# Attention scores of an adjacency-masked network in four 32-column tiles of 96 moving columns

## Chip, cores and metric

The kernel runs on one core of one Trainium2 chip. The metric is the device time of the core in microseconds (us), the median of several executions. Before the change it is 2836.74 us (three runs, 2836.55 to 2839.01).

## What is computed

A pre-norm residual around two layers of masked attention over 128 batches of 64 tokens with 768 features, all in f32:

```python
h = relu(layernorm(x))                              # x: 128 x 64 x 768
for l in range(2):
    m_left, m_right = h @ W_left[l].T, h @ W_right[l].T
    u_left, u_right = h @ m_left^T / sqrt(768), h @ m_right^T / sqrt(768)       # 64 x 64 per batch
    u = u_left * triu(adj) + u_right * triu(adj, 1)^T
    e = exp(u) * adj
    attention = e / (e.sum(2) + 1e-10)
    h = relu(layer_norm(attention @ (h @ W_lin[l].T + b_lin[l])))
out = x + h
```

The left scores are only used on and above the diagonal, the right ones only below it. Half of all score products are thrown away by the mask.

## The kernel before

Each layer has a first pass (left and right projections, scores, softmax) and a second (the linear projection and the attention product). A pass works through 16 stages of 8 batches. In a stage of the first pass, `project` runs 2 x 15 steps of matmuls; after the first step of stage u, `scores(u - 1)` puts a burst of 48 matmuls into the stream of TensorE. What follows on the other engines is cut into tasks, one per half step ("slot"), and `softmax` gives the chain of the scores seven slots. X, Y, Z and V in the profile are the PSUM banks in which the projections are summed, m their copy in SBUF.

```python
def softmax(u):
    return [lambda: next(CHAIN[u], None)] * 7

def project(u, k, just):
    ...
    for i, (at, t, _) in ...:                       # 15 steps
        ...
        for g in range(2):
            for c in range(K2):
                nc.tensor.matmul(p[:, g], w[ORDER[i][0]][:, c, g * P:(g + 1) * P], b()[t][:, c, :], ...)
            if g == 0:
                run(30 * k + 2 * i)                 # tasks of this slot
        if i == 0 and k == 0:
            if u:
                scores(u - 1)
            ...
        read(...)                                   # ACT or DVE takes the bank into m
        run(30 * k + 2 * i + 1)

def scores(u):
    ht, m, adj = HT[1, l, u], M[u], ADJ[u]
    p = ps_aux.tile([P, 2, T], F32, name="aux")[:, 0].rearrange("p (q m) -> p q m", q=Q)
    for q in range(Q):                              # 4 pairs of batches
        for c in range(C):                          # 6 blocks of 128 features
            for h in range(PAIR):                   # 2 batches: column tiles 0-63 and 64-127
                b = q * PAIR + h
                nc.tensor.matmul(p[h * S:(h + 1) * S, q, :], ht[:, c, b * S:(b + 1) * S],
                                 m[:, c, b].rearrange("p k j -> p (k j)"),
                                 start=(c == 0), stop=(c == C - 1))

    def chain():
        wm = sp.tile([P, Q, 2, S], F32, name="wm", bufs=1)
        for k in range(2):                          # adjacency times triangle, on POOL
            nc.gpsimd.tensor_tensor(wm[:, :, k], adj[:, :, 1 - k], tri[:, k]..., op=ALU.mult)
        yield
        flat = wm.rearrange("p q k j -> p (q k j)")
        nc.vector.tensor_tensor(flat, p.rearrange("p q m -> p (q m)"), flat, op=ALU.mult)
        yield
        v = adj[:, :, 0, :]
        nc.vector.tensor_add(v, wm[:, :, 0], wm[:, :, 1])
        yield
        nc.scalar.activation(v, v, AF.Exp, scale=ISTEMPER)
        yield
        ...                                         # times adj, row sums, division, transpose, to DRAM
    CHAIN[u] = chain()
```

The moving data of one matmul are 128 columns: 64 of the left projection, then 64 of the right.

## Time and profile before

| | before |
|---|---|
| time, median | 2836.74 us |
| profiled span | 2835.8 us |
| TensorE busy | 2790.3 us, 98% |
| VectorE (DVE) busy | 1288.6 us, 45% |
| scores (L378): 32 bursts, each | 5.588 us |
| one stage of the first pass | 57.39 us |

A busy TensorE says nothing of gaps inside its stream: its matmuls are pipelined, so their durations overlap, and what they cost is read from their start times. The lines of the page on which the argument rests stand in the prediction. The view of the scores' line (in the second line: total idle us before its records and how often):

```profile
  issue: 10.6, 32
```

One wait of about 0.33 us per burst: that is the entry, where the array changes from 128-column to 64-column tiles (the view takes weight loads and matmuls together; here it is the loads that wait). From the page's list of DMA queues (packets, MB, share of 16 engines):

```profile
q8 instruction: 125, 2.05, 0.3%
```

### The profile page before, as it was taken

The page shows a single profiled execution, that of the slowest core. Times are in us where ns is not written, and L with a number is a line of the kernel's source. Part 1 is how long each engine was busy: PE and PEld are TensorE (multiplying, and loading weights), DVE is VectorE, ACT ScalarE, POOL GpSimd, SP SyncE. Part 2 cuts the span into 40 slices and gives each one's busy share as a digit, 9 for nine tenths or more (in the row PEclk, how much of TensorE's full clock was granted, in tenths as well). Part 3 has the DMA queues.
Part 4 walks back from the last instruction along what each step waited for, and adds up shares of the span by engine and source line. Part 5 has one row for each costly group of instructions (what it writes and reads, how often), then busy time and mean ns, then how long its engine had stood idle before and what let it go on. Part 6 is the DMA issues. An engine that isn't in the chain of part 4 may idle for free.

```text
span 2835.8 us, 39864 instructions
## 1 busy us (share of the span) xinstructions
PE 2790.3 (98%) x15640; PEld 2382.8 (84%) x15640; DVE 1288.6 (45%) x2126; ACT 839.6 (30%) x1453; POOL 1189.4 (42%) x935
## 2 busy tenths in 40 slices
PE   7999999999999999999999999999999999999997
PEld 6888888888888888888778888888888888888885
DVE  6454444444444333332334434343334334666666
ACT  2122222322231244444422221112111224544443
POOL 3343333222322556565422343223322325787875
PEclk9999999999999999999999999999999999999999
DMA  5622443234322243343553432344224304555654
GB/s 155 165 73 73 103 111 77 73 94 119 78 73 75 97 141 117 101 129 104 147 158 88 117 87 73 78 116 97 73 73 103 93 25 127 160 178 160 180 162 125
DMA packets 234043, 310.40 MB, mean 109 GB/s; under 512 B 54144, under 2 KB 184448, under 8 KB 225664
## 3 DMA queue, kind: packets, MB, share of 16 engines
q1 hardware_dynamic: 233568, 307.06, 39.6%
q8 instruction: 125, 2.05, 0.3%
q10 hardware_dynamic: 288, 0.79, 0.1%
q14 instruction: 62, 0.51, 0.1%
HBM read 202.91 MB, written 104.86 MB: 109 GB/s over the span
## 4 chain that ended last, share of the span: by engine, by line
PE 95%; DVE 1%; issue 1%; POOL 1%; ACT 1%; DMA 0%; SPq 0%; DVEq 0%; ACTq 0%; POOLq 0%
PE X L356 23%; PE V L356 15%; PE X L614 12%; PE Y L356 11%; PE Z L356 8%; PE V L614 8%; PE aux L378 6%; PE Y L614 6%; PE Z L614 4%; PE aux L544 3%; POOL w_r L144 1%; DVE m L144 0%; DVE w_l L144 0%; DMA x<-in_x_dram 0%; DVE hl L144 0%
## 5 line engine op out<-in xcount | busy, mean ns | idle before, releaser
L144 POOL TENSOR_TENSOR ts<-ht 128x512 f32<-128x512 f32 x441 | 585.5, 1338 | 1244.6 <-DMA ht<-h 594.5
L189 ACT ACTIVATE m<-X 128x512 f32<-128x512 f32 x256 | 152.8, 597 | 1154.7 <-PE X L356 591.3
L144 POOL TENSOR_TENSOR ts<-ht,ts 128x512 f32<-128x512 f32 x189 | 248.8, 1324 | 156.0 <-PE X L614 78.2
L144 DVE TENSOR_TENSOR m<-m,V 128x512 f32<-128x512 f32 x256 | 174.7, 682 | 283.5 <-PE V L356 282.4
L144 DVE TENSOR_TENSOR m<-m,X 128x512 f32<-128x512 f32 x256 | 163.7, 680 | 274.8 <-PE X L356 274.8
L144 DVE TENSOR_TENSOR m<-m,Z 128x512 f32<-128x512 f32 x128 | 88.0, 687 | 377.1 <-ACT m L189 308.8
L356 PE MATMUL X<-ts,w_l 128*128 128x256 f32 x1024 | 246.1, 384 | 9.7 <-ACT m L189 5.1
L614 PE MATMUL X<-w_n,ts 128*128 128x256 f32 x1024 | 244.0, 380 | 4.1 <-ACT hl L189 3.9
L356 PE MATMUL X<-ts,w_r 128*128 128x256 f32 x1024 | 241.9, 379 | 0.0
L356 PEld LDWEIGHTS X<-ts,w_l 128*128 128x128 f32 x1024 | 194.9, 192 | 40.6 <-issue 6.3
L614 PEld LDWEIGHTS X<-w_n,ts 128*128 128x128 f32 x1024 | 191.7, 190 | 35.0 <-ACT hl L189 4.7
L356 PEld LDWEIGHTS X<-ts,w_r 128*128 128x128 f32 x1024 | 192.3, 190 | 28.7
L255 ACT ACTIVATE ht<-ht,b_col,a_col 128x512 f32<-128x512 f32 x192 | 143.1, 803 | 153.2 <-DMA ht<-h 153.2
L614 PE MATMUL Y<-w_n,ts 128*128 128x256 f32 x768 | 182.4, 379 | 0.0
L356 PE MATMUL Y<-ts,w_l 128*128 128x256 f32 x768 | 181.8, 380 | 0.0
L356 PE MATMUL Y<-ts,w_r 128*128 128x256 f32 x768 | 181.4, 379 | 0.0
L189 ACT ACTIVATE hl<-X 128x512 f32<-128x512 f32 (+1 forms) x136 | 77.7, 572 | 332.7 <-PE X L614 323.1
L378 PEld LDWEIGHTS aux<-m,ht 128*64 128x64 f32 x3072 | 167.0, 137 | 10.6 <-issue 10.6
L378 PE MATMUL aux<-m,ht 128*64 128x128 f32 x3072 | 174.7, 274 | 0.0
L356 PEld LDWEIGHTS Y<-ts,w_l 128*128 128x128 f32 x768 | 146.3, 191 | 20.0
L356 PEld LDWEIGHTS Y<-ts,w_r 128*128 128x128 f32 x768 | 145.9, 190 | 19.8
L614 PEld LDWEIGHTS Y<-w_n,ts 128*128 128x128 f32 x768 | 145.9, 190 | 19.8
(105 smaller groups left out, 4563.1 us busy)
## 6 DMA issues: line engine op xcount, KB each, us to landing
ht<-h SPq DMA_DIRECT2D x63, 1536.0 KB, 7.3
h<-xb SPq DMA_DIRECT2D x124, 384.0 KB, 6.5
z<-z SPq DMA_DIRECT2D x128, 192.0 KB, 2.9
x<-z SPq DMA_DIRECT2D x128, 192.0 KB, 8.5
xr<-in_x_dram SPq DMA_DIRECT2D x128, 192.0 KB, 3.9
out_dram<-xr SPq DMA_DIRECT2D x128, 192.0 KB, 2.7
x<-in_x_dram SPq DMA_DIRECT2D x120, 192.0 KB, 8.5
adj<-in_adj_dram SPq DMA_DIRECT2D x64, 128.0 KB, 2.8
```

The source lines that it names most:

```text
L144: (eng.tensor_add if sign == "+" else eng.tensor_sub)(o, a, b)
L189: nc.scalar.activation(to(o), p, AF.Copy, scale=1.0 if sign == "+" else -1.0)
L255: nc.scalar.activation(ht, ht, AF.Relu, bias=cols[1][:, c:c + 1], scale=cols[0][:, c:c + 1])
L356: nc.tensor.matmul(p[:, g], w[ORDER[i][0]][:, c, g * P:(g + 1) * P], b()[t][:, c, :], start=(new and g == c == 0), stop=(c == K2 - 1), ski ...
L378: nc.tensor.matmul(p[h * S:(h + 1) * S, q, :], ht[:, c, b * S:(b + 1) * S], m[:, c, b].rearrange("p k j -> p (k j)"), start=(c == 0), stop ...
L544: nc.tensor.matmul(cx[k][i, m, :HH], at[j, q, :], hl[j, q, m * HH:(m + 1) * HH], start=True, stop=True)
L614: nc.tensor.matmul(p[:, n], b[t][:, c, r * P:(r + 1) * P], w[s][:, c, :], start=(i in FIRST and i not in PRELOAD and n == c == 0), stop=(c ...
```

## The change

Of the 128 moving columns, rows 0 to 31 of a batch need columns 0 to 95 (all left scores, right ones below token 32), and rows 32 to 63 need columns 32 to 127. So each 64-column tile is cut into two 32-column tiles with 96 moving columns each: a quarter of the products goes. The mask product must then leave out the PSUM columns that were never written, which differ from one 32-partition part to the next, so it becomes four products, and the chain takes an eighth slot. (In `wm` those columns are already zero.)

```diff
             def softmax(u):
-                return [lambda: next(CHAIN[u], None)] * 7
+                return [lambda: next(CHAIN[u], None)] * 8
 ...
-                            nc.tensor.matmul(p[h * S:(h + 1) * S, q, :], ht[:, c, b * S:(b + 1) * S],
-                                             m[:, c, b].rearrange("p k j -> p (k j)"),
-                                             start=(c == 0), stop=(c == C - 1))
+                            mb = m[:, c, b].rearrange("p k j -> p (k j)")
+                            for e in (0, 32):
+                                nc.tensor.matmul(p[h * S + e:h * S + e + 32, q, e:e + 96],
+                                                 ht[:, c, b * S + e:b * S + e + 32], mb[:, e:e + 96],
+                                                 start=(c == 0), stop=(c == C - 1))
 ...
-                    nc.vector.tensor_tensor(flat, p.rearrange("p q m -> p (q m)"), flat, op=ALU.mult)
-                    yield
+                    for i in range(0, P, 32):
+                        r = wm.rearrange("p q k j -> p q (k j)")[i:i + 32, :, i % S:i % S + 96]
+                        nc.vector.tensor_tensor(r, p[i:i + 32, :, i % S:i % S + 96], r, op=ALU.mult)
+                        if i % S:
+                            yield
```

## The prediction

> **What bounds the kernel now.** I began with the busy table and the 40 slices of the page, then took the chain that ended last.
>
> ```profile
> PE 2790.3 (98%) x15640; PEld 2382.8 (84%) x15640; DVE 1288.6 (45%) x2126; ACT 839.6 (30%) x1453; POOL 1189.4 (42%) x935
> ...
> PE 95%; DVE 1%; issue 1%; POOL 1%; ACT 1%; DMA 0%; SPq 0%; DVEq 0%; ACTq 0%; POOLq 0%
> PE X L356 23%; PE V L356 15%; PE X L614 12%; PE Y L356 11%; PE Z L356 8%; PE V L614 8%; PE aux L378 6%; PE Y L614 6%; PE Z L614 4%; PE aux L544 3%; POOL w_r L144 1%; DVE m L144 0%; DVE w_l L144 0%; DMA x<-in_x_dram 0%; DVE hl L144 0%
> ```
>
> TensorE carries 95% of the chain; everything else runs beside it. The scores (aux, L378) are 6% of it. So a microsecond taken from the scores is a microsecond of the end time, and DVE time counts only where it delays a PSUM bank that TensorE wants back. The ceiling is low: all scores cost 6%, and the change removes a quarter of their columns.
>
> The groups by line and the views of single lines give the operations touched:
>
> ```profile
> L378 PE MATMUL aux<-m,ht x3072: 272/273/324, 84.4 to 2349.3; 128*64 128x128 f32 x192
> L544 PE MATMUL aux<-hl,at x1024: 482/482/534, 979.0 to 2822.2; 64*64 64x384 f32 x171
> L390 DVE TENSOR_TENSOR wm<-aux,wm x32: 681/683/693, 115.0 to 2349.7; 128x512 f32<-128x512 f32 x32
> L393 DVE TENSOR_TENSOR adj<-wm x32: 419/424/426, 115.7 to 2350.4; 128x256 f32<-128x256 f32 x32
> ```
>
> A matmul's 273 ns is a pipelined latency, not its cost. The cost is in the start times, so I read the timeline of TensorE around one of the 32 scores bursts:
>
> ```profile
> 369.69 1.89 PE L356 MATMUL X<-ts,w_l 128*128 128x256 f32 x8
> 371.51 5.46 PE L378 MATMUL aux<-m,ht 128*64 128x128 f32 x96
> 376.90 1.99 PE L356 MATMUL Z<-ts,w_l 128*128 128x256 f32 x8
> ```
>
> 48 matmuls of the program are 96 records (two per f32 matmul). Record by record, inside a burst they start in pairs, one in each 64-column tile: 7 ns between the two, 102 ns to the next pair, so 109.3 ns a pair. A 256-column matmul on the whole array starts every 215.9 ns, and the four 64x64 tiles of the context (L544, 384 columns) start 6.7 ns apart and repeat every 322.6 ns. The three lie on one line: period = 2.6 ns + 0.8333 ns x columns, whether one, two or four tiles are at work. The entry costs 93 ns (309 ns from the last X start instead of 216) and 51 ns at the second pair; leaving costs 93 and 104 ns. Altogether each burst adds 5.588 us between X and the second Z matmul (48 x 109.3 ns + 0.34 us), and all 32 bursts agree within 1 ns. In a steady stage of the first pass (57.388 us from burst to burst) no other gap appears.
>
> **What the Trainium skill says.**
> - "TensorE: Matmul & The Clock Gate", section "Measured speedup vs the span model": column tiles of 32 and row tiles run concurrently, about 4 ns per further tile; a full 4x4 packing is listed with 10.6 times. The trace agrees in kind with 6.7 to 7 ns per tile, for two and four tiles. It holds no 32-column tile and no four column tiles.
> - "TensorEngine Tiling (Array Packing)", section "Key Properties": a change of tiling mode drains the array. The trace agrees: about 0.3 us a burst, and the change keeps it, one entry and one exit per burst.
> - The same page, section "Instruction Overhead": about 60 cycles per matmul, so a small moving size stops paying. At 96 columns we are above this, and the trace's own fixed term is 2.6 ns.
> - "VectorE: DVE Perf Modes", section "The TRN2 errata — SBUF-src ops pay a fixed extra latency per instruction": an f32 tensor_tensor takes (N+151)/0.96 ns, N per partition. That gives 691 and 424 ns for 512 and 256; the trace has 683 and 424. Partitions don't enter, so a quarter of the partitions is no cheaper.
>
> **The change part by part.**
>
> *Matmuls.* Per burst 96 matmuls of 32x96 in place of 48 of 64x128; in records 192 for 96. The program order of the changed kernel has exactly this in the same places, the same two waits inside, nothing else moved on TensorE. The four tiles of one (q, c) follow each other (h=0: 0 and 32, h=1: 64 and 96), so four records can run at once: still 48 groups, each 2.6 + 0.8333 x 96 = 82.6 ns instead of 109.3. 48 x 26.7 = 1.28 us a burst, x 32 = **-41.0 us**. Entry and exit: kept; four starts at about 7 ns are 28 ns, inside 82.6.
>
> Can instructions be fed that fast? Needed is one program matmul per 41 ns. Semaphore waits of TensorE's sequencer are recorded when it reaches them, and where two stand four program matmuls apart they are as little as 126 ns apart (51 ns of it the wait itself), under 32 ns a matmul. So yes.
>
> *Mask product.* One 128x512 product of 0.683 us becomes four of 32 partitions x 384: (384+151)/0.96 = 557 ns each (interpolating the trace's 424 and 683: 553). 4 x 0.555 = 2.22 us, +1.54 us a burst, +49 us of DVE busy in all. It hides or doesn't, by place:
> - Steady stages, layer 0: the product follows the V read of the previous pass part; then DVE was idle 2.82 us until the Z read. The extra 1.5 us fits. The exp with its 1.28 us table load moves behind the Z read on ACT; the next X read then ends at about 408.5 where TensorE wants the bank at 408.64. Hidden, barely.
> - Steady stages, layer 1: the chain takes a slot more, so exp now comes after the Y read and the product-and-sum ahead of the X reads. The timeline before:
>
> ```profile
> 1843.68 0.69 DVE L144 TENSOR_TENSOR m<-m,V 128x512 f32<-128x512 f32 x1 [2.70 <-PE V L356]
> 1844.28 0.68 DVE L390 TENSOR_TENSOR wm<-aux,wm 128x512 f32<-128x512 f32 x1
> 1845.00 0.42 DVE L393 TENSOR_TENSOR adj<-wm 128x256 f32<-128x256 f32 x1
> ...
> 1847.13 0.60 ACT L189 ACTIVATE m<-Y 128x512 f32<-128x512 f32 x1 [0.82 <-PE Y L356]
> ...
> 1848.86 1.29 DVE L144 TENSOR_TENSOR m<-m,X 128x512 f32<-128x512 f32 x2 [0.76 <-PE X L356]
> ```
>
> The Y read ends at 1847.73, exp (0.42) at 1848.16, product and sum (0.42 each) at 1849.07: the X reads start 0.2 us late, and they end at 1850.36, when the next X weights wanted to load at 1850.17. A stall of 0.13 to 0.2 us (estimate), 14 stages: **+2 us**.
> - End of each first pass: scores, softmax and the second pass's first reads follow one another, and ACT reads X only after exp.
>
> ```profile
> 954.03 0.60 ACT L189 ACTIVATE hl<-X 128x512 f32<-128x512 f32 x1 [2.38 <-DVE wm L407]
> ...
> 954.68 1.99 PE L614 MATMUL X<-w_n,ts 128*128 128x256 f32 x8 [1.13 <-ACT hl L189]
> ```
>
> Back-to-back independent DVE operations start 0.08 us before the former's end, so the four take about 2.0 us and the chain is 1.3 us later: layer 0 stalls 1.3 us more. Layer 1 (no wait before; exp would end at 2352.6, the read at 2353.2, wanted at 2352.85) about 0.4. **+1.7 us**.
>
> Sum: -41.0 + 2 + 1.7 = -37.3 us; 2836.7 - 37.3 = **2799 us**, 1.3% less.
>
> **The rivals.**
> 1. Four column tiles don't overlap fully: each tile of the full 128 rows needs its own moving stream, four per partition where the trace shows two (64x128 pairs, and 64x64 quads that share rows). If only two run at once, a group is 2 x 82.6 = 165 ns: +56 ns x 48 x 32 = +86 us, 2922 us, slower by 3%. If bandwidth sets the old rate of 109 ns, nothing is won: about 2840. For it: no 32-column tile in the trace. Against it: the skill's 16-tile figure needs four column streams, and the fixed term of 2.6 ns was the same with one, two and four tiles.
> 2. Weight loads bound: 128 columns of weights per group stay, now in less time. If the loads of the tiles were served one after another at the 53 ns that a 64-column load takes by its start times (107 ns for both), the old burst sat at that bound by accident, and the group stays at 107: 2838 us. Against it: the pair's loads start 7 ns apart and the context's four (64 columns each) did too.
> 3. DVE takes the bound: every stage stalls for the 1.5 us. At 30 stages that is +45 us and eats all: 2844 us. Against it: DVE is 45% busy and the idle times above; only layer 1's one place and the pass ends have no room.
>
> **Range and chances.** The gain can't exceed 41 us by much (1.5%; entry may save 27 ns a burst more, under 1 us), so "faster by over 2%" needs something unseen: 0.02. Two at a time, or serial, is the way to slower by 2%: 0.05. Stalls of DVE or ACT that I mis-sized (0 to 15 us) set the upper edge: 2791 to 2814 us.
>
> **What would show it.** The scores' group: 6144 records of 128*32 with 96 columns, busy time about 134 us where it was 174.7; starts in fours, 7 ns apart, 83 ns from four to four; burst to burst 56.1 us in layer 0 and 56.2 to 56.3 in layer 1. DVE busy about 1337 us, each mask product near 0.555 us. TensorE's waits for ACT hl about 1.7 us longer, and a new wait of X for DVE m in layer 1. If the fours start 100 ns or more apart, rival 1 or 2 holds and I am wrong on the mechanism; if they are at 83 but the stage stays above 56.7, rival 3.

## More of the kernel before

TensorE's longer waits before (us in total, times, longest):

```profile
PE X L614 <- ACT hl L189: 3.9, 2, 2.7
...
PE V L356 <- DVE m L144: 2.0, 2, 1.5
...
PE X L356 <- DVE m L144: 0.2, 1, 0.2
```

## The result and the profile after

After: **2814.15 us** (median of 6 runs, 2812.97 to 2815.35), before in the same rounds 2836.64 us (6 runs, 2835.55 to 2839.01). The ratio is 0.992, 95% interval 0.9907 to 0.9933: less than 2%. Ratios here are the mean time of one kernel's fast runs over that of the other's of the same rounds, so not quite the ratio of the medians quoted. The results are correct. The time stands on the upper edge of the range (2814.15 us against 2814, nearer than the runs agree among themselves): 15 us above the central number, and the gain is 22 us where 37 were expected.

The page of the kernel after (span; busy us, share and instructions per engine; the instruction queue; the chain that ended last):

```profile
span 2811.2 us, 46104 instructions
...
PE 2755.9 (98%) x18712; PEld 2343.6 (83%) x18712; DVE 1338.1 (48%) x2222; ACT 838.0 (30%) x1453; POOL 1189.7 (42%) x935
...
q8 instruction: 149, 2.44, 0.4%
...
PE 94%; DVE 2%; issue 1%; DMA 1%; POOL 1%; ACT 1%; SPq 0%; DVEq 0%; ACTq 0%; POOLq 0%
```

TensorE still carries the chain. DVE's busy time is 1338.1 us where about 1337 were expected. TensorE has 3072 more matmul and 3072 more weight-load records, and the instruction queue 24 packets more: 6144 / 24 = 256 instructions a packet, and 2.44 MB / 149 = 16.4 kB a packet. (The trace's 38110 instructions of TensorE make 149 such blocks, so this queue is TensorE's.)

The view of the scores' line, and of the mask product (count, ns of one low/median/high, first and last start; then the idle time before, us and times):

```profile
L382 PE MATMUL aux<-m,ht x6144: 242/246/270, 83.9 to 2323.3; 128*32 128x96 f32 x199
...
  issue: 17.4, 48
...
L396 DVE TENSOR_TENSOR wm<-aux,wm x128: 537/553/565, 116.5 to 2325.3; 32x384 f32<-32x384 f32 x128
```

The product takes 553 ns as interpolated. But the scores' records have 48 waits for "issue", of loads and matmuls together, where they had 32: 16 are new. The timeline of TensorE shows two kinds of burst. One without a new wait (start, length, matmuls):

```profile
1811.37 1.89 PE L356 MATMUL X<-ts,w_l 128*128 128x256 f32 x8
1813.19 4.17 PE L382 MATMUL aux<-m,ht 128*32 128x96 f32 x192
1817.29 1.99 PE L356 MATMUL Z<-ts,w_l 128*128 128x256 f32 x8
```

From 1813.19 to 1817.29 is 4.10 us; the same distance before was 5.39 us. Record by record the starts come in fours, 7 ns apart, with 82.6 ns from four to four. Altogether such a burst adds 4.294 us between X and the second Z matmul, where 5.588 - 1.28 = 4.30 was worked out.

And a burst of the same kernel one stage on:

```profile
1867.72 1.67 PE L356 MATMUL X<-ts,w_l 128*128 128x256 f32 x7
1869.32 4.00 PE L382 MATMUL aux<-m,ht 128*32 128x96 f32 x182
1873.97 0.52 PE L382 MATMUL aux<-m,ht 128*32 128x96 f32 x10 [0.65 <-issue]
1874.42 1.78 PE L356 MATMUL Z<-ts,w_l 128*128 128x256 f32 x7
```

After 182 matmuls TensorE stands still for 0.65 us, and nothing that the profile shows holds it back: no semaphore, no engine. Ten matmuls are left. What the DMA engines did from 1869 to 1874.2 us (40 slices of 0.13 us, busy tenths; then packets and queues):

```profile
DMA  0000000000000000000040000000000000000000
...
DMA packets 1, 0.02 MB, mean 3 GB/s; under 512 B 0, under 2 KB 0, under 8 KB 0
...
q8 instruction: 1, 0.02, 1.2%
```

One packet only, on the instruction queue. In the trace it runs from 1871.63 to 1872.59 us (the view books it to the slice in which it starts; 1.2% of 16 engines' 5.2 us is the same 1.0 us). The matmuls resume 1.38 us after its end. 13 of the 32 bursts have such a gap, of 0.16 to 1.0 us, 5.9 us in all; the other 19 are exact to some ns. Two more stand outside the bursts. The first burst, with its wait behind the burst:

```profile
83.93 4.17 PE L382 MATMUL aux<-m,ht 128*32 128x96 f32 x192
88.03 1.35 PE L356 MATMUL Z<-ts,w_l 128*128 128x256 f32 x5
92.28 0.92 PE L356 MATMUL Z<-ts,w_l 128*128 128x256 f32 x3 [2.91 <-issue]
```

Here the instruction packet ran from 89.909 to 90.925 us, and the matmul came 1.36 us after. In all 14 waits that I could match with a packet (13 bursts and this one), matmuls resume 1.23 to 1.46 us after its end, 2.24 to 2.88 us after its start; over all 149 packets, one took 0.88 to 1.44 us.

TensorE's waits after, as above for before:

```profile
PE X L621 <- ACT hl L189: 5.7, 3, 2.8
...
PE V L356 <- DVE m L144: 4.1, 3, 1.5
...
PE Z L356 <- issue: 2.9, 1, 2.9
PE aux L382 <- issue: 2.2, 5, 0.7
...
PE X L356 <- DVE m L144: 1.2, 1, 1.2
```

ACT hl (the end of the first passes) has grown by 1.8 us, DVE m before V by 2.1 and before X by 1.0; the two "issue" lines are new. (The list leaves out short waits, so 2.2 us for the bursts is less than the 5.9 by start times.) The end of the first pass in layer 0:

```profile
941.96 0.60 ACT L189 ACTIVATE hl<-X 128x512 f32<-128x512 f32 x1 [2.38 <-DVE wm L414]
...
942.61 1.99 PE L621 MATMUL X<-w_n,ts 128*128 128x256 f32 x8 [2.70 <-ACT hl L189]
```

The wait is 2.70 us where it was 1.13: 1.57 more, where 1.3 was expected.

**The balance of the two profiles**, by start times. The span fell by 24.6 us (2835.8 to 2811.2), 12.7 less than the predicted 37.3.

| place | predicted, us | measured, us |
|---|---|---|
| 32 bursts | -41.0 | -35.5 (-41.4 without the gaps of 5.9) |
| wait for instructions outside the bursts (Z behind the first) | 0 | +3.1 |
| steady stages of layer 1 | +2 | +0.5 (14 x 0.035) |
| pass ends | +1.7 | +2.0 (1.57 and 0.46) |
| stage with layer 1's exp table load; V waiting for DVE m, at 194 and at 398 us; one X | 0 | +3.5 (0.97; 1.34, 0.90; 0.26) |
| rest | 0 | +1.8 |
| sum | -37.3 | -24.6 |

Half of the rest, 0.94 us, is a stretch at 1396 us in which matmuls start 427 ns apart instead of 216 (half clock) after a wait of 3.1 us; the other half lies among the context's matmuls at 2795 us. Such stretches stand in other places from run to run.

The wait of V at 194 us can be mistaken for one for instructions, since a packet ended 1.37 us before it. But the timeline puts 1.18 us of it down to DVE m. It is there, with 0.3 to 1.3 us, in all seven runs that have the eighth slot, also in the one below that changes nothing but the slot, and in none of the seven with seven slots, stalled bursts or not. So it belongs to the slot.

So the trace points at the supply of instructions, 5.9 + 3.1 = 9.0 us. The Trainium skill, "Runtime: NRT & Kernel Launch", section "Instruction fetch mechanics", says that each engine's instruction memory is a queue refilled in blocks of 16 KiB, 256 instructions, that the next block is fetched while the present one runs, and that this is "mostly hidden". The size agrees with 256 per packet above. That it is hidden doesn't hold here, if the reading is right. An f32 matmul of the program is four instructions (two weight loads, two matmuls). In the projections, where a matmul record starts every 216 ns, a block lasts 128 x 0.216 = 27.6 us; in the old burst 128/96 of 48 x 109.3 ns, 7.0 us; in the new one 128/192 of 48 x 82.6 ns, 2.64 us. By the count that follows, 2.65 to 3.43 us pass in the 13 stalled bursts from the first matmul of a block to the resumption (the packet starts 0.2 to 1.0 us into the block, and 2.24 to 2.88 follow). Old bursts have room to spare; new ones have none. Which bursts stall fits too: I counted TensorE's instructions from the start of the program. (The trace holds none of those that run ahead of the program's own; the count puts 49 there, which no view shows. What the positions have to each other doesn't depend on it.) The stalled bursts begin at positions 116 to 193 within a block of 256, none of the others there; those that begin at 103 or lower or at 208 or higher are exact. In 12 of the 13 the long gap stands at the same place, 16 or 17 instructions ahead of the end of the second block that the burst touches. That explains the lower end: with 384 instructions a burst gets as far as there, about 497, only if it begins at 113 or later. At the upper end the packets' times differ: in the stalled bursts the packet starts 0.9 to 2.3 us into the burst; in those that begin at 208 to 234 one starts 0.9 to 3.0 us ahead of the burst, while the projections still run.

### The profile page after: what moved, and what is told of

It reads as the page before. It is cut to its first block, busy times and chain, and to the rows that moved or that the text cites. A ratio compares the mean times of both kernels' runs of the same rounds, so it can differ in the third digit from the quotient of the medians.

```text
span 2811.2 us, 46104 instructions
## 1 busy us (share of the span) xinstructions
PE 2755.9 (98%) x18712; PEld 2343.6 (83%) x18712; DVE 1338.1 (48%) x2222; ACT 838.0 (30%) x1453; POOL 1189.7 (42%) x935
## 3 DMA queue, kind: packets, MB, share of 16 engines
q8 instruction: 149, 2.44, 0.4%
## 4 chain that ended last, share of the span: by engine, by line
PE 94%; DVE 2%; issue 1%; DMA 1%; POOL 1%; ACT 1%; SPq 0%; DVEq 0%; ACTq 0%; POOLq 0%
PE X L356 23%; PE V L356 15%; PE X L621 12%; PE Y L356 11%; PE Z L356 8%; PE V L621 8%; PE Y L621 6%; PE aux L382 5%; PE Z L621 4%; PE aux L551 3%; POOL w_r L144 1%; DVE m L144 0%; DMA z<-z 0%; DVE wm L396 0%; DMA x<-in_x_dram 0%
## 5 line engine op out<-in xcount | busy, mean ns | idle before, releaser
L590 POOL TENSOR_TENSOR z<-z,b 128x768 f32<-128x768 f32 x64 | 115.4, 1814 | 95.4 <-DVE z L587 95.4
L144 DVE TENSOR_TENSOR hl<-hl,X 128x512 f32<-128x512 f32 (+1 forms) x136 | 83.2, 653 | 146.2 <-PE X L621 144.3
```

The lines of the kernel that those rows point to most:

```text
L144: (eng.tensor_add if sign == "+" else eng.tensor_sub)(o, a, b)
L590: nc.gpsimd.tensor_add(zs[k], zs[k], rows["b"])
```

## The experiments

Theory F: the missing time is mostly the supply of instructions, which depends on how many instructions TensorE consumes in how short a time and on where the burst falls in the blocks. Theory D, the rival: it is the longer mask product and the slot it takes, in whatever place. A third (T): four column tiles are in themselves slower or cause gaps, whatever their rate. "Before" was run beside each; medians of 2838.31, 2837.55 and 2837.02 us in three groups of nine runs.

### The product alone, on the kernel before

```diff
-                    nc.vector.tensor_tensor(flat, p.rearrange("p q m -> p (q m)"), flat, op=ALU.mult)
-                    yield
+                    for i in range(0, P, 32):
+                        ...                        # four parts as in the change; softmax * 8
```

> The kernel before with only the mask product of the change (four parts of 32 partitions, the chain a slot longer), old score matmuls. Theory F (the missing gain is TensorE waiting for its own instructions inside the denser bursts; the product costs only at the pass ends and where layer 1's exp table load moves): all 32 bursts stay at 5.588 us, total 2 to 6 us above before, 2839 to 2843 us. Rival D (the four-part product and the slot shift give back the 17 us): 2850 to 2854 us.

Measured: 2845.66 us (2844.51 to 2848.21) against 2838.31, ratio 1.0028 (1.0015 to 1.0040). That is +8 us by the ratio: between the two expectations, so D holds for more than I gave it and for less than all. All bursts are 5.588 us, with no gap. TensorE's waits in this kernel:

```profile
PE X L617 <- ACT hl L189: 6.1, 3, 3.1
...
PE V L356 <- DVE m L144: 3.1, 3, 1.5
...
PE X L356 <- DVE m L144: 1.2, 1, 1.2
```

By start times: pass ends +1.57 and +0.46 as in the change, the stage with the table load +0.97, V about +0.9, layer 1's stages 0.5 together, and two stretches at half clock, 8 records each, 16 x 0.21 = 3.4 us. This adds up to 7.8 us (smaller differences of both signs are left out, among them 0.3 of V at 192 us).

### The new matmuls with the old product

The product runs over all of the PSUM tile again; since a quarter of it is no longer written by matmuls, ACT writes zeros over it first. The edit is against the changed kernel.

```diff
-                return [lambda: next(CHAIN[u], None)] * 8
+                return [lambda: next(CHAIN[u], None)] * 7
 ...
+                nc.scalar.activation(p, tri.rearrange("p k j -> p (k j)").unsqueeze(1).to_broadcast([P, Q, 2 * S]),
+                                     AF.Copy, scale=0.0)
 ...
-                    for i in range(0, P, 32): ...  # four parts
+                    nc.vector.tensor_tensor(flat, p.rearrange("p q m -> p (q m)"), flat, op=ALU.mult)
+                    yield
```

> The changed kernel's matmuls with the old single product over 128 partitions and the old seven slots; ACT writes zeros over the scores' PSUM tile first (32 times about 0.6 us in ACT's slack), since the corner that no matmul writes is now read. Theory F: the stalls inside the bursts stay (6 us inside, some 4 us at two places just outside), the rest of what was given back goes: 2804 to 2808 us. Rival D: all of the 41 us appears, 2795 to 2798 us.

Measured: 2807.04 us (2806.85 to 2807.27), ratio 0.9891 (0.9876 to 0.9906), correct. As F had it: 31 us gained, not 41. 13 bursts are stalled again, 32 bursts take 143.2 us together (143.3 in the change), and the wait of Z behind the first is 2.88 us. The pass end is back at 1.39 us and layer 1's stages are 56.095 us, the 57.388 less one burst's gain. With no part of D left, the loss of 10 us stays.

### As few columns, but half the instructions

Two 64-column tiles as before, with 96 columns each. This gives a wrong result (relative error 0.027), but it streams as many columns as the change with 192 instructions a burst instead of 384. The edit is against the kernel before.

```diff
-                            nc.tensor.matmul(p[h * S:(h + 1) * S, q, :], ht[:, c, b * S:(b + 1) * S],
-                                             m[:, c, b].rearrange("p k j -> p (k j)"),
+                            nc.tensor.matmul(p[h * S:(h + 1) * S, q, :96], ht[:, c, b * S:(b + 1) * S],
+                                             m[:, c, b].rearrange("p k j -> p (k j)")[:, :96],
 ...                                                # product on the same 96 columns, one instruction
```

> Wrong on purpose: the old two tiles of 64 columns, but only the first 96 moving columns, product over these 96 in one instruction. A burst takes as long as the changed kernel's ideal (48 times 82.6 ns) with half of its instructions (192). Theory F: no burst stalls, each adds about 4.3 us, time 2794 to 2798 us. Rival (short moving columns or the shorter stage as such cause the stalls): gaps inside bursts as in the changed kernel, 2804 us or more.

Measured: 2796.96 us (2794.95 to 2797.8), ratio 0.9854 (0.9841 to 0.9868). All bursts are 4.308 us and none has a gap. The scores' line shows the entry waits only:

```profile
L378 PE MATMUL aux<-m,ht x3072: 245/246/298, 82.2 to 2308.2; 128*64 128x96 f32 x192
...
  issue: 10.6, 32
```

It is 10 us faster than the run above, with as many columns: the number of instructions is what differs (and the four tiles, which the next run takes, and off TensorE ACT's zeros and a narrower product, 128x384 in 550 ns; that these cost nothing here is not shown by itself).

### Four tiles, all 128 columns, on the kernel before

```diff
+                            for e in (0, 32):
+                                nc.tensor.matmul(p[h * S + e:h * S + e + 32, q, :],
+                                                 ht[:, c, b * S + e:b * S + e + 32], mb, ...)
```

> Correct result: four tiles of 32 columns as in the changed kernel, but all 128 moving columns, single product, old slots. As many instructions a burst as the changed kernel (384), in the old kernel's 5.25 us. If four column tiles run as freely as two: groups of four every 109.3 ns, a burst of 5.55 to 5.59 us. A block of 256 instructions lasts 3.5 us instead of 2.66, so theory F has stalls at most a few tenths of a us in a few bursts: 2836 to 2842 us. If doubling the instructions costs by itself, whatever the pace: bursts of 6 us and more, 2848 us or above.

Measured: 2839.57 us (2836.11 to 2841.69), ratio 1.0007 (0.9995 to 1.0020), correct. 384 instructions a burst and four tiles, and no gap in any burst; the bursts take 5.575 us, the fours start 109.3 ns apart.

```profile
L380 PE MATMUL aux<-m,ht x6144: 272/273/298, 82.3 to 2350.0; 128*32 128x128 f32 x199
...
  issue: 10.6, 32
```

So T falls: neither four tiles nor 384 instructions cost by themselves. The bursts begin at the same positions as in the change, 116 to 193 among them. Here a block lasts 128/192 of 48 x 109.3 ns, 3.5 us, a little longer than the 3.43 us that the slowest supply took above. It is the rate that counts, and the limit lies between 2.6 and 3.5 us a block. One wait for instructions is left, outside the bursts: Z behind the first one, 1.30 us (3.07 in the change).

### Shifting the blocks under the bursts

If the position within a block decides, then instructions that do nothing, put ahead of all bursts, must change *which* bursts stall. Eighty increments of a semaphore that nobody waits for ("empties") were put into TensorE's stream once, at the start. This was a single look, of unknown state, so only its bursts are used, not its time (2817.01 us).

```diff
+    pad = tc.alloc_semaphore('pad')
 ...
+            for _ in range((80, 0)[l]):
+                nc.tensor.sem_inc(pad, 1)
```

> The changed kernel with 80 empty instructions once, at the very start of TensorE's queue. Every burst's position in its block of 256 instructions moves by 80. In the changed kernel the bursts that stalled inside started at positions 116 to 193 of a block, and no other did. Theory F: now the bursts number 1, 3, 8, 13, 15, 21, 26, 28 and 31 stall (positions 183, 137, 150, 163, 117, 155, 168, 122, 181), number 6 or 22 (196, 214) hardly, and those that stalled before (4, 9, 11, 14, 17, 19, 22, 24, 27, 29) do not unless they are on this list. A stall bound to the stage, its data or its DMAs keeps the old numbers. No clear change of the time: 2810 to 2818 us.

Observed: bursts 1, 3, 6, 8, 13, 15, 21, 26, 28 and 31 are longer (burst 1 by 4.5 us, the others by 0.08 to 0.9), all others exact. The nine named in advance stalled, burst 22 didn't, and burst 6, named as "hardly", did by 0.35 us. Bursts 4, 9, 11, 14, 17, 19, 22, 24, 27 and 29, ten of those that stall in the change, are free. With the same matmuls, the same product and the same slots, this is the strongest sign: only F says anything of the position. The gaps stand at the same place in the block again, about 497 by the count.

### Moving all bursts to free positions: two misses in time

A stage of the change has 873 instructions on TensorE; 23 empties make it 896 = 3.5 blocks, so bursts alternate between two positions. The first try put 91 empties at the start, 80 together at the start of layer 1 and one in each of the first 23 steps of a stage.

> The changed kernel with empty instructions added on TensorE's queue (91 at the start of the first pass of layer 0, 80 at that of layer 1, 23 a stage spread over the steps), so that every burst starts at position 218 or 90 (last one 72) of the 256 instructions of a block and never in 116 to 193, where all stalled bursts started. Nothing else changes. Theory F: no gap inside any burst, time 8 to 11 us below the changed kernel's 2814, 2803 to 2806 us, although 827 instructions more are run. Rival D, or stalls of another cause: 2813 us or more.

Measured: 2813.91 us (2812.78 to 2814.82), ratio 0.9915 (0.9901 to 0.9928). A miss: no faster. But the bursts did what was meant: 31 of 32 are 4.294 to 4.295 us. The time went elsewhere, as the waits show:

```profile
PE aux L295 <- issue: 14.8, 1, 14.8
PE X L357 <- issue: 10.9, 1, 10.9
```

A row of 91 empties holds up the first transposes, and one of 80 holds up the first X of layer 1 for 11 us where the change waits 5. An empty costs some 0.15 us when nothing hides it.

The second try spread the 80 over the second pass, put two more in each step of stage 1 (60), and 159 at the start, so that the first burst stands at a free position too.

> As e6_aligned (which had no gap inside 31 of 32 bursts, but lost 6 us where its 80 empty instructions stood together at the start of layer 1), with these 80 spread over the second pass of layer 0, and with the first burst moved to position 32 of its block, so that the block's end falls well after the burst that meets the weights' DMAs. Theory F: no burst of the 32 stalls, 2801 to 2805 us, 9 to 13 below the changed kernel's 2814. If the empty instructions cost as much as they save, or the stalls' cause is another: 2811 us or more.

Measured: 2817.92 us (2817.02 to 2818.47), ratio 0.9932 (0.9919 to 0.9944). No burst has a gap for instructions (the first ran at half clock), but 159 empties in a row stand on the path:

```profile
PE aux L299 <- issue: 25.2, 1, 25.2
```

25.2 us / 159 = 0.158 us each; in the trace they start 0.151 us apart. The first burst starts at 95.2 us instead of 83.9, some 11 us later, and that is what it lost. The same with the old product:

> e2_one_product (single product, PSUM tile zeroed by ACT) with the same added empty instructions as e8_aligned_spread. If fetch stalls and product are the two causes and add up: e2's 2807 less its stalls of 10 us or so, 2795 to 2799 us, close to the full gain of 41 us. If they overlap: 2802 us or more.

Measured: 2808.29 us (2807.45 to 2811.54), ratio 0.9902 (0.9887 to 0.9917), all 32 bursts exact, the same loss at the start. My expectation of these three runs forgot that an instruction that does nothing still takes its turn.

### The same positions, with the empties hidden

All empties are now behind matmuls: six or seven a step in stage 0, three or two in stage 1, one in the first 23 steps of every other stage, and one in each of 80 steps of layer 0's second pass.

```diff
                         if g == 0:
+                            s30 = 15 * k + i
+                            pads(6 + (s30 < 2) if (l, u) == (0, 0) else
+                                 2 + (s30 < 23) if (l, u) == (0, 1) else int(s30 < 23))
                             run(30 * k + 2 * i)
 ...                                                # second pass
+                            if not last and u and 15 * (u - 1) + i < 80:
+                                pads(1)
```

> e8_aligned_spread again, with the 159 empty instructions of its start (they took 25.2 us, 0.158 us each, and held the first matmul up by 12 us) spread over the first stage, six or seven a step, where TensorE's sequencer runs ahead. Otherwise the changed kernel. Theory F: no burst stalls, and no longer start: 2803 to 2808 us, 7 to 11 below the changed kernel's 2814 to 2815. If empty instructions cost TensorE time wherever they stand: 2812 us or more.

Measured: **2804.13 us** (2803.03 to 2805.53), ratio 0.9883 (0.9870 to 0.9897), correct. All 32 bursts are 4.294 or 4.295 us (137.4 us together, 143.3 in the change). The burst that stood still at 1873 us is now

```profile
1862.99 4.17 PE L390 MATMUL aux<-m,ht 128*32 128x96 f32 x192
1867.08 1.99 PE L361 MATMUL Z<-ts,w_l 128*128 128x256 f32 x8
```

1035 instructions more and 10 us less. Its control, the same empties in the kernel before:

> Control: the kernel before with the same empty instructions at the same places. It has no stalled burst, so under theory F there is nothing to win: within 2 us of before. If the empty instructions help or hurt by themselves: off by 4 us or more.

Measured: 2836.14 us (2835.32 to 2837.77), ratio 0.9997 (0.9985 to 1.0010). The empties are worth nothing where no burst is short of instructions. So it is no effect of having them that would show in the old bursts too.

### The slot alone, on the kernel before

```diff
                     nc.vector.tensor_tensor(flat, p.rearrange("p q m -> p (q m)"), flat, op=ALU.mult)
                     yield
+                    yield                          # and softmax * 8
```

> The kernel before with nothing changed but one empty slot in the softmax chain after the product (eight slots). e1_product_parts, with the slot and the four-part product, was 7 to 8 us slower than before. If the shift of the slots is what costs (exp and its table load at another place, the idle tasks one slot on): 2 to 5 us above before; if it is the longer product alone: within 1 us of before.

Measured: 2842.22 us (2839.04 to 2843.61) against 2837.55, ratio 1.0016 (1.0003 to 1.0028): +4.5 us for an empty task. The pass end is unchanged at 1.30 us (it has no slots there), but V's waits for DVE m and the stage with the table load behave as in the change:

```profile
PE V L356 <- DVE m L144: 4.0, 3, 1.5
...
PE X L356 <- DVE m L144: 1.1, 1, 1.1
```

By start times some 3 us of the 4.5 are in these: V at 192 us +1.21 (the wait that the change has at 194 us), V at 401 us +0.90, the table load +0.85. The first burst runs partly at half clock (+0.82), and the rest isn't placed.

### The best version

The new matmuls in four tiles, the old product (with ACT's zeros), seven slots, and the hidden empties.

> e7_best with its start instructions spread likewise: single product, zeroed tile, no stalled burst. If fetch stalls and product with its slot are the two causes and add up: 2794 to 2799 us (e7's 2808 less 12 us of start), about 41 us under before, which is what the prediction's 32 bursts of 1.28 us come to. If they overlap: 2802 us or more.

Measured: **2796.52 us** (2794.04 to 2800.76), ratio 0.9861 (0.9846 to 0.9876), correct: 1.4% faster than before, and about as fast as the kernel with half the instructions. It beats both kernels, by less than 2%.

```profile
L392 PE MATMUL aux<-m,ht x6144: 246/246/270, 82.2 to 2305.7; 128*32 128x96 f32 x199
...
  issue: 10.6, 32
```

Set beside the run with the same empties and the four-part product, 2804.13 - 2796.52 = 7.6 us (6.2 by the ratios) is what the product in parts and its slot cost, much as on the kernel before (8).

## Why the prediction was right, and where it was wrong

- **What bounds the kernel: right.** TensorE's stream sets the end; the gain came from the scores' starts alone.
- **Matmuls, -41.0 us: right in mechanism and size, where instructions are there.** The fours start 82.6 ns apart, the line of 2.6 ns + 0.8333 ns x columns holds for four 32-column tiles at 96 and at 128 columns, and entry and exit stayed. With all bursts free, they give 178.8 - 137.4 = 41.4 us.
- **"Can instructions be fed that fast? ... So yes.": this step failed.** It was read from semaphore waits four matmuls apart, which shows how fast a few instructions leave the sequencer, but not how fast new ones arrive. A burst of 384 instructions runs through a block in 2.64 us, and the supply took 2.65 to 3.43 in the stalled ones. The trace gives 9.0 us for it. The runs agree: 10.0 us come back when only the positions change (2814.15 to 2804.13; the two were measured in different groups, by the ratios 0.9920 and 0.9883 it is 10.5, each known to about 4 us; the two profiled spans differ by 9.2), nothing comes back on the kernel before, and no burst loses anything at 3.5 us a block. My upper edge of 2814 was justified by stalls of DVE or ACT alone. That the time came out on it is luck: more than half of what is missing has another cause, for which the prediction had allowed nothing.
- **Mask product: each instruction right (553 ns against 555), layer 0 hidden as said.** Layer 1's steady stages were mis-sized, 14 x 0.035 = 0.5 us where +2 stood. The pass ends were right in kind: 1.57 and 0.46 where 1.3 and 0.4 stood.
- **The slot: left out.** It was followed through the steady stages only. The stage in which layer 1's exp loads its table (+0.97) and two places in layer 0 where V waits for DVE (+1.34 and +0.90) weren't looked at. With what follows from it at half clock, product and slot cost some 8 us (run on the kernel before) where 3.7 stood.
- **Rivals 1 and 2: refuted** by the 82.6 ns and by the run with four tiles at 128 columns. (The 53 ns that rival 2 reads from the loads' start times are 55 in the trace.) **Rival 3: refuted** in the steady stages (56.095 and 56.13 us, below the 56.7 that was named), true only in the few places above.

Open: the stretches at half clock follow waits of 2.5 us and more (not every such wait has one) and wander between runs, so some 2 us of the balance are not assigned to a part of the change. What asks for a block is not settled. The range of positions that stall, 116 to 193, was read from one trace and foretold the next; its lower end follows from the place of the gap, and at its upper end the packet is seen to start ahead of the burst, but no run isolates what starts it, nor why the wait ends some 16 instructions ahead of a block's end. Why the packet behind the first burst came so late (it ended at 90.9 us, while the weights of the second pass filled the DMA queues) was not isolated either.

## What to carry to other kernels

Cutting a matmul into more, smaller tiles saves array time but multiplies instructions: beside the columns, work out how long a block of 256 instructions lasts in the densest stretch, and compare it with the time from a block's first instruction to the end of the wait for the next block (here 2.65 to 3.43 us: no burst stalled at 3.5 us a block, 13 of 32 did at 2.64). If it is short, look at where the stretch falls in the blocks before giving up the idea: some 1000 cheap instructions in the right places (23 in most stages) were worth as much here as a quarter of the change. And splitting an elementwise operation by partitions costs its full time for each part (553 ns for 32x384 here, 550 for 128x384), while one more task slot delays everything behind it: follow it through the stages that aren't steady too.

## What the Trainium skill lacked or had wrong

- "Runtime: NRT & Kernel Launch", section "Instruction fetch mechanics": fetching is called "mostly hidden" because the sequencer dispatches more slowly than blocks are filled. Here it is not: 9 to 10 us of 2814 where 384 instructions come in 4.3 us; 13 of 32 bursts stall by 0.16 to 1.0 us.
- The same section gives TensorE room for 2048 instructions and, further on, speaks of two lines of 256. With room for 2048, if it were kept full, a burst of 384 would not run dry behind 27.6 us a block; the runs behave as with the two lines.
- No page that I found gives the time from a packet's end to the matmul that had waited: 1.23 to 1.46 us in 14 waits, 2.24 to 2.88 from the packet's start.
- No page that I found gives what a bare semaphore increment costs in TensorE's own stream: they start 0.151 us apart (159 of them took 25.2 us) where no matmul hides them.
- "TensorE: Matmul & The Clock Gate", section "Measured speedup vs the span model", lists three column tiles beside the full packing, and no four with all 128 rows: here, in f32, four such tiles run at once, 7 ns apart, 82.6 ns from four to four at 96 columns and 109.3 at 128.
